# The scan's layer normalisation: from a shared job of ScalarE and GpSimd to two VectorE instructions

## The chip, the cores and the metric

The kernel runs on one core of one Trainium2 chip. The metric is the device time of one execution in microseconds. The engines are called PE (TensorE matmul), PEld (TensorE weight load), DVE (VectorE), ACT (ScalarE), POOL (GpSimd) and SP (SyncE, which here only issues DMAs).

## The reference, cut to what matters

The input `x` is 32 sequences of 256 tokens with 256 channels. A conditioned state-space block works on it first, then two layers of local attention and a gated feed-forward block work on the block's output, and `x` is added at the end. The change touches the layer normalisation in the first block alone:

```python
xc = silu(conv(x @ W_in.T + t_emb))                 # 512 channels
mu, var = xc.mean(-1), xc.var(-1)
xn = (xc - mu) / sqrt(var + 1e-05) * ln_g + ln_b    # the normalisation that is changed
Bm, Cm, dt = split(xn @ W_xproj.T, 3)               # 16 states
Ad, Bd = 1 + tanh(dt @ W_dt.T + b_dt)*0.01 * A,  Bm * min(norm(xn), 1)
h = clip(h*Ad + Bd*xn, -10, 10)                     # step by step over 256 tokens
y = (Cm . h + D*xn) * silu(gate) @ W_out.T
```

`xn` is needed by the recurrence, by the skip term `D*xn` and, through its length, by `Bd`. `Bm`, `Cm` and `dt` are not computed from `xn` but from raw sums over `xc`, corrected afterwards with two figures of each token: the reciprocal standard deviation r and the shift -mu*r.

## The kernel before, in words

**Groups and chunks.** The 32 sequences are four groups of eight (`NG`, `GB`), and the scan of a group runs over 256 time steps in eight chunks of 32 (`CH`). The state of a group is one tile of 128 partitions (16 states by 8 sequences) by 512 channels. A chunk holds 8 x 32 = 256 tokens, and so two blocks of 128 tokens (`NJ` = 2): there are 4 x 8 x 2 = 64 normalisations in all, one for each group, chunk c and block j.

**Stages.** Group 0 is scanned alone (`alone` is true for it), while TensorE also projects the inputs of the other groups ahead. After that attention and feed-forward of one group run beside the scan of the next group. At the end attention and feed-forward of group 3 run without a scan.

**What sets the order.** Every piece of work of the scan is a small function that is put into a slot with `at(slot, function, ...)`. There is one slot for each time step; `s0 = c * CH` is a chunk's first one. Attention and feed-forward have stages of their own (eight for a sequence), and the scan's slots are dealt out between them. The program that arises goes to a scheduler, which may move an instruction against others; where a call is wrapped in `tc.keep_in_program_order`, that instruction keeps its place. On the chip each engine works through its own queue in order.

**The recurrence.** `load_rows` (L685) reads one row of `xn` of eight sequences from DRAM (`xnd`), spread over the 16 states; it is put six slots ahead of its step and writes to one of six `xrep` buffers. `scale_row` (L706) multiplies it by `beta` on ACT, and `step` (L716) makes the new state on DVE with a custom instruction. `read_out` (L728) multiplies the states on PE. In group 0 two of each eight rows come from TensorE (`spread_rows`, L693) instead of a DMA.

**One normalisation before the change.** For block j of chunk c the slots are counted from s = s0 - 26 + 4j.
- s: `norm_turn` transposes the block on PE into a PSUM bank, `tp_x` (L548). All PSUM tiles of the kernel share one tag with eight banks.
- s+2: `norm_stats` takes mean and variance on DVE (L558, L560), adds epsilon (L562), takes the power -1/2 on POOL (L565) and negates the mean on DVE (L567).
- s+5: `norm_shift` makes -mu*r on ACT (L572), and `norm_apply` reads the bank on ACT and writes r*x - mu*r to the SBUF tile `xn` (L579).
- s+6: `norm_affine` multiplies `xn` by the weight `lng_sb` (L586) and adds the offset `lnb_sb` (L587), both on POOL.
- s+9: `norm_out` writes `xn` to DRAM through SP's queue (L591), and ACT squares and sums it for the length (L593).
- At s0 - 11 `length` takes the root of the sum (L599, L600). At s0 - 9 `figures` spreads r, -mu*r and the length over the tokens (L609), and at s0 - 7 `figures_in` makes `beta` and the other coefficients.

`norm_apply` and both instructions of `norm_affine` work on 128 x 512 elements, `norm_shift` on 128 x 1.

Of the kernel before, what the change touches and what calls it, by code (L numbers as in the profile page):

```python
# [10 lines left out]
FP = mybir.dt.float32  # L11
BF = mybir.dt.bfloat16
I32 = mybir.dt.int32
AF = mybir.ActivationFunctionType
ALU = mybir.AluOpType
# [4 lines left out]
P = 128  # L20
# [12 lines left out]
NJ = GB * CH // P  # L33
# [19 lines left out]
def bc(ap, axis, n):  # L53

    ap = ap.unsqueeze(axis)
    shape = list(ap.shape)
    shape[axis] = n
    return ap.broadcast_to(shape)
# [15 lines left out]
def kernel(  # L74
# [29 lines left out]
    nc = tc.nc  # L104
# [5 lines left out]
    def loaded(src, shape, name, q=None):  # L110
        t = const.tile(shape, FP, tag=name, name=name)
        (q or nc.scalar).dma_start(out=t, in_=src)
        return t
# [26 lines left out]
    lng_sb = loaded(s_ln_g.partition_broadcast(P), [P, DI], "lng_sb")  # L140
    lnb_sb = loaded(s_ln_b.partition_broadcast(P), [P, DI], "lnb_sb")
# [80 lines left out]
    def program(ctx, exact):  # L222
# [3 lines left out]
        sm = ctx.enter_context(tc.tile_pool(name="sm", bufs=2, reuse_waits="tile"))  # L226
# [7 lines left out]
        def bank(pool, tag, name):  # L234
            return pool.tile([P, DI], FP, tag=tag, name=name)
# [141 lines left out]
        def group_scan(g):  # L377
# [8 lines left out]
            alone = g == 0  # L386
# [3 lines left out]
            ck = [{} for _ in range(NCH)]  # L390

            def at(s, what, *args):
                agendas[-1].setdefault(s, []).append(partial(what, *args))
# [146 lines left out]
            def norm_turn(c, j):  # L540
                if j == 0:
                    ck[c]["xnd"] = dp.tile([GB * CH, DI], FP, tag="xnd", name="xnd")

                    ck[c]["stat"] = sm.tile([P, NJ, 3], FP, tag="stat", name="stat")
                    ck[c]["ss"] = sm.tile([P, NJ], FP, tag="ss", name="ss")
                tp = bank(ps_w, "w", "tp_x")
                for ch in range(NC_):
                    nc.tensor.transpose(  # L548
                        tp[:, ch * P : (ch + 1) * P],
                        ck[c]["xc"][:, ch, j * P : (j + 1) * P],  # L550
                        ident,
                    )
                ck[c]["tp", j] = tp

            def norm_stats(c, j):
                tp, stat = ck[c]["tp", j], ck[c]["stat"]
                st = sm.tile([P, 6], FP, tag="st", name="st")
                nc.vector.bn_stats(st, tp)  # L558
                mv = sm.tile([P, 2], FP, tag="mv", name="mv")
                nc.vector.bn_aggr(mv, st)  # L560
                ve = sm.tile([P, 1], FP, tag="ve", name="ve")
                nc.vector.tensor_scalar_add(  # L562
                    ve, mv[:, 1:2], LN_EPS if alone else 4 * LN_EPS
                )
                nc.gpsimd.tensor_tensor(stat[:, j, 0:1], ve, neg_half[:, 0:1], ALU.pow)  # L565
                nm = sm.tile([P, 1], FP, tag="nm", name="nm")
                nc.vector.tensor_scalar_mul(nm, mv[:, 0:1], -1.0)  # L567
                ck[c]["nm", j] = nm

            def norm_shift(c, j):  # L570
                stat = ck[c]["stat"]
                nc.scalar.activation(  # L572
                    stat[:, j, 1:2], ck[c].pop(("nm", j)), AF.Copy, scale=stat[:, j, 0:1]
                )

            def norm_apply(c, j):
                tp, stat = ck[c].pop(("tp", j)), ck[c]["stat"]
                xn = sp.tile([P, DI], FP, tag="xn", name="xn", bufs=2)
                nc.scalar.activation(  # L579
                    xn, tp, AF.Identity, bias=stat[:, j, 1:2], scale=stat[:, j, 0:1]  # L580
                )
                ck[c]["xn", j] = xn

            def norm_affine(c, j):
                xn = ck[c]["xn", j]
                nc.gpsimd.tensor_mul(xn, xn, lng_sb)  # L586
                nc.gpsimd.tensor_add(xn, xn, lnb_sb)  # L587

            def norm_out(c, j):
                xn = ck[c].pop(("xn", j))  # L590
# [10 lines left out]


            def figures(c):
                stat = ck[c].pop("stat")
                ck[c]["rhs"] = []
                for j in range(NJ):
                    rhs = sm.tile([P, 3, CH], FP, tag="rhs", name="rhs")
                    tc.keep_in_program_order(
                        nc.vector.tensor_mul(rhs, bc(tok_step, 1, 3), bc(stat[:, j], 2, CH))  # L609
                    )  # L610
                    ck[c]["rhs"].append(rhs)
# [244 lines left out]
            for c in range(NCH):  # L856
                s0 = c * CH
                for hb in range(CH // TB):
                    s = s0 + hb * TB
                    for i in range(NI):  # L860
                        at(s + 4 * i + 5, read_out, c, hb, i)
                    at(s + 21, gated, c, hb)
                    at(s + 25, out_gate, c, hb)
                    at(s + 11, skip, c, hb)
                for ch in range(NC_):
                    at(s0 - 38 + 2 * ch, conv_in, c, ch)
                    at(s0 - 37 + 2 * ch, conv_taps, c, ch)
                    at(s0 - 36 + 2 * ch, conv_th, c, ch)
                    if not alone:
                        at(s0 - 35 + 2 * ch, conv_out, c, ch)  # L870
                for ch, s in enumerate((13, 16, 17, 18)):
                    at(s0 + s + 2, gate_th, c, ch)
                    if not alone:
                        at(s0 + s + 4, gate_out, c, ch)
                at(s0 - 25, raw_copy, c)
                at(s0 - 24, raw_turn, c)
                for j in range(NJ):
                    s = s0 - 26 + 4 * j
                    at(s + 2, norm_stats, c, j)
                    at(s + 5, norm_shift, c, j)  # L880
                    at(s + 5, norm_apply, c, j)
                    at(s + 6, norm_affine, c, j)
                    at(s + 9, norm_out, c, j)
                at(s0 - 11, length, c)
                at(s0 - 9, figures, c)
                at(s0 - 7, figures_in, c)
                at(s0 - 6, decay_th, c)
                at(s0 - 5, decays, c)
                at(s0 - 4, put_c, c, 0)
                at(s0 + 4, put_c, c, 1)  # L890
                for d in range(KM):
                    at(s0 + 45 + 2 * d, copy_y, c, d)
                    at(s0 + 46 + 2 * d, put_y, c, d)
            agendas.append({})
            for c in range(NCH):
                s0 = c * CH
                at(s0 - 43 if alone else s0 + 6, load_x, c)
                if alone:
                    for ch in range(NC_):
                        at(s0 - 40 + 2 * ch, project, c, ch)  # L900
                else:
                    for i in range(2):
                        at(s0 - 44 + 2 * i, load_projected, c, i)
                for ch, s in enumerate((13, 16, 17, 18)):
                    at(s0 + s, project, c, NC_ + ch)
                at(s0 - 27, raw_sums, c)
                for j in range(NJ):
                    at(s0 - 26 + 4 * j, norm_turn, c, j)
                at(s0 - 8, figures_out, c)
                for t in range(CH):  # L910
                    if not by_tensor(t):
                        at(s0 + t - 6, load_rows, c, t)
                    if by_tensor(t) and t % XR == 0:
                        at(s0 + t - 4, spread_rows, c, t)
                    at(s0 + t - 2, scale_row, c, t)
                for hb in range(CH // TB):
                    s = s0 + hb * TB
                    at(s - 9 if alone else s + 7, load_skip, c, hb)
                    at(s + 23, out_turn, c)
                for d in range(KM):  # L920
                    at(s0 + 43 + 2 * d, project_y, c, d)

            if alone:
                n = (NG - 1) * NCH * 2
                for u in range(n):
                    s = -30 + u * (NCH * CH) // n
# [6 lines left out]
        def scan_slots(groups):  # L933


            slots, scans = {}, [group_scan(g) for g in groups]
            for part in range(2):
                for i, agendas in enumerate(scans):
                    for s, what in agendas[part].items():
                        slots.setdefault(i * S + s, []).extend(what)  # L940
            for s in range(min(slots), max(slots) + 1):
                for what in slots.get(s, ()):
                    what()
                yield s
# [717 lines left out]
```

## Time and profile before

| | |
|---|---|
| median of three runs | 3595.93 us (3587.54 to 3600.59) |
| profiled execution | 3582.75 us, of which the span is 3581.0 us |
| granted TensorE clock | 0.992 |
| PE busy | 3446.0 us, 96% of the span |
| PEld busy | 2253.9 us, 63% |
| DVE busy | 2667.3 us, 74% |
| ACT busy | 1998.7 us, 56% |
| POOL busy | 1892.2 us, 53% |

The first scan step (L716) of group 0 starts 47.5 us into the span, the first step of group 1 at 436.7 us, and the last step of group 3 at 2795.8 us. What comes before 40 us is the start, 40 to 440 us is the scan alone, 440 to 2700 us the scan beside attention and feed-forward, and the rest is attention and feed-forward alone.

A busy share is an average over these stages, so a stage has to be looked at by itself. PE's ends are modelled, so a PE that is shown as busy is not always one at its peak. In a line on a group of instructions the columns are: line, engine, operation, output and inputs, shape, count, then the busy time and the mean of one, then the idle time of the engine just before them with what ended it. In a line on waits they are the time in total, how often, and the longest one.

### The profile page before, as it was taken

What the parts mean: (1) busy time and instruction counts of PE and PEld (TensorE: products, weight loads), DVE (VectorE), ACT (ScalarE), POOL (GpSimd) and SP (SyncE); (2) the same over time, 40 slices, a digit from 0 to 9 for tenths busy, and PEclk for the clock granted to TensorE, in tenths of its full rate; (3) what the DMA queues carried; (4) which work ended last, traced back from release to release, by engine and by line L of the source; (5) the groups of instructions that cost most, each with busy time, mean ns of one, the idle gap of its engine ahead of it and who ended that gap; (6) DMA issues with size and microseconds to landing.
All of it is one profiled execution on the core that took longest, in us unless ns stands there. A gap on an engine that the chain in (4) does not pass through costs nothing.

```text
span 3581.0 us, 57673 instructions
## 1 busy us (share of the span) xinstructions
PE 3446.0 (96%) x20220; PEld 2253.9 (63%) x20220; DVE 2667.3 (74%) x5049; ACT 1998.7 (56%) x3599; POOL 1892.2 (53%) x1842
## 2 busy tenths in 40 slices
PE   7999989999999999999999999999999999999999
PEld 4555335666656666666666666666666677777777
DVE  5888889888788777888787778888877555555553
ACT  4666656656555665566566655655666444434442
POOL 4433477645556555655565556555544454544551
PEclk9999999999999999999999999999999999999999
DMA  7887665445354545444454555534454112011101
GB/s 207 219 221 213 198 174 149 120 117 143 109 144 125 149 141 148 130 118 127 118 142 125 138 149 140 143 106 131 114 141 122 54 50 61 13 30 38 33 27 37
DMA packets 468767, 435.68 MB, mean 122 GB/s; under 512 B 228723, under 2 KB 308084, under 8 KB 468340
## 3 DMA queue, kind: packets, MB, share of 16 engines
q1 hardware_dynamic: 384018, 419.88, 42.0%
q10 hardware_dynamic: 84450, 12.01, 2.0%
q8 instruction: 163, 2.67, 0.3%
q14 instruction: 136, 1.11, 0.1%
HBM read 383.54 MB, written 46.66 MB: 120 GB/s over the span
## 4 chain that ended last, share of the span: by engine, by line
PE 61%; DVE 19%; DMA 7%; POOL 6%; ACT 4%; issue 3%; SPq 0%; ACTq 0%; DVEq 0%; POOLq 0%
PE ps_qkv L989 13%; PE pa L1375 13%; DVE h L716 7%; PE po_f L1402 7%; DMA xrep<-xnd 5%; PE ps_wo L1039 5%; PE y L728 4%; PE ov L1271 4%; PE sc L1215 3%; PE ps_out L808 3%; PE ps_in L399 2%; PE tr_qk L1028 2%; PE rs L1252 2%; ACT xrep L706 2%; DVE acc L489 2%
## 5 line engine op out<-in xcount | busy, mean ns | idle before, releaser
L716 DVE CUSTOM_DVE_ANT_0 h<-h,xrep,lim 128x512 f32<-128x512 f32 x1024 | 961.0, 938 | 228.9 <-ACT xrep L706 196.6
L706 ACT ACTIVATE xrep<-xrep,beta 128x512 f32<-128x512 f32 x960 | 672.3, 718 | 341.4 <-DMA xrep<-xnd 219.8
L989 PE MATMUL ps_qkv<-qkv,res 128*128 128x512 f32 x1536 | 713.5, 601 | 17.9 <-DVE rinv L1260 8.4
L1375 PE MATMUL pa<-hT,w 128*128 128x256 f32 (+1 forms) x2816 | 675.1, 382 | 11.3 <-DVE zT L799 10.7
L1375 PEld LDWEIGHTS pa<-hT,w 128*128 128x128 f32 (+1 forms) x2816 | 516.9, 188 | 152.9 <-issue 35.4
L1013 POOL TENSOR_TENSOR rot<-rot,swp 128x512 f32<-128x512 f32 x256 | 339.9, 1328 | 475.3 <-DVE swp L1010 423.5
L1021 POOL TENSOR_TENSOR rn<-ss,neg_half 128x8 f32<-128x8 f32 x256 | 466.8, 1823 | 18.4 <-DVE ss L1019 7.8
L989 PEld LDWEIGHTS ps_qkv<-qkv,res 128*128 128x128 f32 x1536 | 282.2, 191 | 301.6 <-issue 241.4
L728 PE MATMUL y<-h,ly 128*32 128x512 f32 x2048 | 348.9, 609 | 16.9 <-DVE h L716 13.9
L1327 POOL TENSOR_TENSOR rstd<-ve,neg_half 128x2 f32<-128x2 f32 x64 | 46.9, 733 | 527.6 <-DVE ve L1325 511.3
L1393 DVE SCALAR_TENSOR_TENSOR ag<-pa,b_sb,ag 128x256 f32<-128x256 f32 x320 | 151.6, 474 | 222.4 <-ACT ag L1386 222.3
L1402 PE MATMUL po_f<-ag,w 128*128 128x256 f32 x1280 | 309.0, 389 | 5.9 <-DVE fo L1413 3.8
L1022 POOL TENSOR_TENSOR rot<-rot,rn 128x512 f32<-128x512 f32 x256 | 289.4, 1130 | 20.0
L1402 PEld LDWEIGHTS po_f<-ag,w 128*128 128x128 f32 x1280 | 236.8, 191 | 71.3 <-issue 12.0
L1386 ACT ACTIVATE ag<-pa,b_sb 128x256 f32<-128x256 f32 x320 | 150.2, 469 | 233.1 <-PE pa L1375 232.1
L1002 ACT ACTIVATE sq<-ps_qkv 128x512 f32<-128x512 f32 x256 | 150.8, 595 | 185.1 <-PE ps_qkv L989 119.4
L1039 PE MATMUL ps_wo<-oT,wo 128*128 128x256 f32 x1024 | 231.7, 379 | 0.5 <-DVE ag L1393 0.5
L489 DVE SCALAR_TENSOR_TENSOR acc<-xr,wc_sb,acc 128x256 f32<-128x256 f32 x384 | 195.1, 531 | 47.7 <-POOL acc L478 47.2
L1005 DVE TENSOR_TENSOR rot<-ps_qkv,rc_sb 128x512 f32<-128x512 f32 x256 | 174.8, 683 | 65.6 <-ACT sq L1002 65.0
L1039 PEld LDWEIGHTS ps_wo<-oT,wo 128*128 128x128 f32 x1024 | 194.4, 190 | 28.1 <-DVE ag L1393 0.9
L1227 ACT ACTIVATE pT<-sc 128x512 f32<-128x512 f32 x384 | 202.3, 603 | 7.6 <-PE sc L1215 5.8
L1271 PE MATMUL ov<-pT,v_sb 128*64 128x256 f32 (+1 forms) x2048 | 183.7, 330 | 19.4 <-DVE ag L1393 19.3
(160 smaller groups left out, 5482.8 us busy)
## 6 DMA issues: line engine op xcount, KB each, us to landing
xrep<-xnd SPq DMA_DIRECT2D x960, 256.0 KB
rb<-inv SPq DMA_DIRECT2D x128, 256.0 KB
xnd<-xn SPq DMA_DIRECT2D x64, 256.0 KB
qkv<-in_wqkv_dram SPq DMA_DIRECT2D x24, 512.0 KB
ahead<-xs_a SPq DMA_DIRECT2D x48, 256.0 KB
xp<-ahead SPq DMA_DIRECT2D x48, 256.0 KB
xd<-xnd SPq DMA_DIRECT2D x192, 64.0 KB
w<-in_w_dram SPq DMA_DIRECT2D x80, 128.0 KB
```

The lines of the kernel that those rows point to most:

```text
L489: nc.vector.scalar_tensor_tensor(acc, xr[:, :, k : k + CH], wc_sb[:, ch, k : k + 1], acc, ALU.mult, ALU.add,)
L706: scaled = nc.scalar.activation(bx, ck[c].pop(("bx", t), bx), AF.Copy, scale=ck[c]["beta"][:, t : t + 1])
L716: nc.vector._custom_dve(TENSOR_ADD_SAT, out=h_new, in0=state["h"], in1=bx, s0=ck[c]["lim"][:, 0, t : t + 1], s1=ck[c]["lim"][:, 1, t : t + 1],
L728: nc.tensor.matmul(ck[c]["y", hb][32 * q : 32 * q + 32, :], ly[hb % 2][:, 32 * t : 32 * t + 32], ck[c].pop(("h", hb * TB + t)), start=(i = ...
L989: nc.tensor.matmul(ps, res[b][:, k, t0 : t0 + W], wt["qkv", a][:, k], start=(k == 0), stop=(k == KM - 1),)
L1013: nc.gpsimd.tensor_add(rot, rot, swp)
L1021: nc.gpsimd.tensor_tensor(rn, ss, neg_half, ALU.pow)
L1022: nc.gpsimd.tensor_mul(rot, rot, bc(rn, 2, DH))
L1039: nc.tensor.matmul(po[:, d], wt["wo", 0][:, c, d * P : (d + 1) * P], oT[:, c, :], start=(c == 0), stop=(c == NC_ - 1),)
L1271: nc.tensor.matmul(ov[r * DH : (r + 1) * DH, i, kw * W :], self.qkv[b][2][:, kw, h * DH : (h + 1) * DH], self.p.pop((b, kw, i0 + i, r)), s ...
L1375: nc.tensor.matmul(dst[x], wt["w1", m][:, k, x], self.h[:, k], start=(k == 0), stop=(k == KM - 1),)
L1402: nc.tensor.matmul(self.po[:, d], wt["w2", 0][:, m, d * P : (d + 1) * P], self.ag[m], start=(m == 0), stop=(m == len(MCH) - 1),)
```

## The change

The two POOL instructions and the two ACT instructions of a normalisation are taken out. Two DVE instructions of the form (in0 op scalar) op in1 take their place:
- In `norm_stats`, slot s+2, DVE reads the bank and writes (x - mu) * weight to `xn`. This does not need r, so it doesn't wait for POOL's power. The bank is free after it.
- In the new `norm_scale` DVE makes `xn` * r + offset in place. It stands at slot s+5 in group 0 and at slot s+7 in the other groups, and it keeps its place in the program's order.

The negated mean (L567) goes too. Its product with r, which `figures` needs, is made for both blocks of a chunk at once by one small DVE instruction in `figures`. For that, mean and variance are kept for the chunk in a tile `mv` of 128 x 2 x 2. The power on POOL (L565), `norm_out` and all other slots stay.

```diff
             def norm_stats(c, j):
-                tp, stat = ck[c]["tp", j], ck[c]["stat"]
+                tp, stat, mv = ck[c]["tp", j], ck[c]["stat"], ck[c]["mv"][:, j]
                 st = sm.tile([P, 6], FP, tag="st", name="st")
                 nc.vector.bn_stats(st, tp)
-                mv = sm.tile([P, 2], FP, tag="mv", name="mv")
                 nc.vector.bn_aggr(mv, st)
...
                 nc.gpsimd.tensor_tensor(stat[:, j, 0:1], ve, neg_half[:, 0:1], ALU.pow)
-                nm = sm.tile([P, 1], FP, tag="nm", name="nm")
-                nc.vector.tensor_scalar_mul(nm, mv[:, 0:1], -1.0)
-                ck[c]["nm", j] = nm
-
-            def norm_shift(c, j):
-                stat = ck[c]["stat"]
-                nc.scalar.activation(
-                    stat[:, j, 1:2], ck[c].pop(("nm", j)), AF.Copy, scale=stat[:, j, 0:1]
-                )
-
-            def norm_apply(c, j):
-                tp, stat = ck[c].pop(("tp", j)), ck[c]["stat"]
                 xn = sp.tile([P, DI], FP, tag="xn", name="xn", bufs=2)
-                nc.scalar.activation(
-                    xn, tp, AF.Identity, bias=stat[:, j, 1:2], scale=stat[:, j, 0:1]
+                nc.vector.scalar_tensor_tensor(
+                    xn, ck[c].pop(("tp", j)), mv[:, 0:1], lng_sb, ALU.subtract, ALU.mult
                 )
                 ck[c]["xn", j] = xn
 
-            def norm_affine(c, j):
+            def norm_scale(c, j):
                 xn = ck[c]["xn", j]
-                nc.gpsimd.tensor_mul(xn, xn, lng_sb)
-                nc.gpsimd.tensor_add(xn, xn, lnb_sb)
+                tc.keep_in_program_order(
+                    nc.vector.scalar_tensor_tensor(
+                        xn, xn, ck[c]["stat"][:, j, 0:1], lnb_sb, ALU.mult, ALU.add
+                    )
+                )
...
             def figures(c):
-                stat = ck[c].pop("stat")
+                stat, mv = ck[c].pop("stat"), ck[c].pop("mv")
+                nc.vector.scalar_tensor_tensor(
+                    stat[:, :, 1], mv[:, :, 0], -1.0, stat[:, :, 0], ALU.mult, ALU.mult
+                )
...
                     at(s + 2, norm_stats, c, j)
-                    at(s + 5, norm_shift, c, j)
-                    at(s + 5, norm_apply, c, j)
-                    at(s + 6, norm_affine, c, j)
+                    at(s + 5 if alone else s + 7, norm_scale, c, j)
                     at(s + 9, norm_out, c, j)
```

More of the change, by code (lines that the diff above doesn't have):

```diff
@@ L545, in norm_turn @@
                     ck[c]["ss"] = sm.tile([P, NJ], FP, tag="ss", name="ss")
+                    ck[c]["mv"] = sm.tile([P, NJ, 2], FP, tag="mv", name="mv")
                 tp = bank(ps_w, "w", "tp_x")
```

## The prediction

> **What bounds the kernel now.** I read the busy table by stage first, because the page's shares mix four regimes (columns: stretch, its length, then busy us of each engine, granted clock, DMA share, GB/s).
>
> ```profile
> core 0: us, PE busy (x) PEld busy (x) DVE busy (x) ACT busy (x) POOL busy (x), PEclk, DMA share, GB/s
> 40.00:440.00 400.00, 371.59 (x1567) 187.49 (x1567) 343.64 (x616) 255.04 (x465) 163.59 (x216) 0.97 0.77 211
> 440.00:740.00 300.00, 277.68 (x1586) 158.35 (x1586) 266.42 (x483) 184.27 (x341) 189.10 (x180) 0.98 0.54 148
> 740.00:1500.00 760.00, 726.22 (x4450) 475.58 (x4447) 609.61 (x1159) 450.72 (x819) 431.89 (x420) 0.99 0.49 134
> 1500.00:2700.00 1200.00, 1171.54 (x7303) 779.52 (x7302) 960.37 (x1825) 722.23 (x1313) 687.24 (x638) 1.00 0.48 130
> ```
>
> Group 0's scan (40 to 440 us) has DVE at 86%; in this stretch the chain of work is led by DVE's scan step (23%) and the row loads (20%). From 1500 us on PE is at 98% and DVE at 80%: PE sets the pace. 440 to 1500 lies between. After 2700 no normalisation is left.
>
> Next the groups of instructions, for prices.
>
> ```profile
> L716 DVE CUSTOM_DVE_ANT_0 h<-h,xrep,lim 128x512 f32<-128x512 f32 x1024 | 961.0, 938 | 228.9 <-ACT xrep L706 196.6 <-DVE h L716 8.7 <-PE y L728 2.3
> L586 POOL TENSOR_TENSOR xn<-xn,lng_sb 128x512 f32<-128x512 f32 x64 | 92.0, 1437 | 88.4 <-ACT xn L579 88.4
> L587 POOL TENSOR_TENSOR xn<-xn,lnb_sb 128x512 f32<-128x512 f32 x64 | 88.9, 1390 | 4.4
> L579 ACT ACTIVATE xn<-tp_x,stat 128x512 f32<-128x512 f32 x64 | 49.7, 777 | 2.1 <-ACT stat L572 0.4
> L572 ACT ACTIVATE stat<-nm,stat 128x1 f32<-128x1 f32 x64 | 18.7, 293 | 148.7 <-POOL stat L565 146.6 <-DMA rw<-raw 2.1
> L567 DVE TENSOR_SCALAR nm<-mv 128x1 f32<-128x1 f32 x64 | 8.9, 140 | 0.0
> L1393 DVE SCALAR_TENSOR_TENSOR ag<-pa,b_sb,ag 128x256 f32<-128x256 f32 x320 | 151.6, 474 | 222.4 <-ACT ag L1386 222.3
> L1005 DVE TENSOR_TENSOR rot<-ps_qkv,rc_sb 128x512 f32<-128x512 f32 x256 | 174.8, 683 | 65.6 <-ACT sq L1002 65.0
> L1010 DVE TENSOR_TENSOR swp<-ps_qkv,rs_sb 128x256 f32<-128x256 f32 x512 | 191.7, 415 | 1.9 <-POOL rot L1013 1.2
> ```
>
> Then the timeline around one normalisation of group 0, DVE above POOL, for what the two engines do to each other:
>
> ```profile
> 211.69 0.80 DVE L716 CUSTOM_DVE_ANT_0 h<-h,xrep,lim 128x512 f32<-128x512 f32 x1
> 212.53 1.78 DVE L716 CUSTOM_DVE_ANT_0 h<-h,xrep,lim 128x512 f32<-128x512 f32 x1
> ...
> 212.49 1.26 POOL L586 TENSOR_TENSOR xn<-xn,lng_sb 128x512 f32<-128x512 f32 x1 [1.56 <-ACT xn L579]
> 213.84 1.60 POOL L587 TENSOR_TENSOR xn<-xn,lnb_sb 128x512 f32<-128x512 f32 x1
> ```
>
> The scan step beside L586 takes 1.78 us and not 0.80. It is no accident: the 348 scan steps that overlap no POOL instruction have a median of 0.808 us, and the stretched ones lie beside POOL's two-input instructions. DVE instructions with a PSUM input don't stretch (L779: 0.670 to 0.687 us in all 64). Summed over 40 to 440 us, what DVE instructions took over their undisturbed time beside L586 or L587 is 22.7 us (29 cases); over 440 to 2700 it is 11.3 us (15 cases).
>
> Last the waits, ACT's and SP's own:
>
> ```profile
> ACT stat L572 <- POOL stat L565: 146.6, 44, 8.3
> SPq L591 <- POOL xn L587: 149.9, 46, 7.1
> ```
>
> ACT stands 3.3 us at a time before `norm_shift`, SP as long before writing `xn`.
>
> **The change part by part.** *Prices.* The first new DVE instruction reads the bank. Its form costs 474 ns on 256 elements (L1393); 256 more cost 683 - 415 = 268 ns (L1005, L1010); so 0.742 us, and with a PSUM input it shouldn't stretch. The second reads two SBUF tensors. The same form on 256 elements has undisturbed medians of 0.418 (L773) and 0.478 us (L489), so 0.69 to 0.75; I take 0.72. It can stretch: scan steps of 440 to 2700 us gained 0.136 us on average, so I add 0.12 there. The small product in `figures` I take at 0.2 us a chunk (L656 0.164, L636 0.234, similar forms).
>
> [...]
>
> *Start (before 47.5 us), 2 normalisations.* Here the chain is bare: block 1's epsilon ends at 31.49 us, POOL's power waits behind block 0's L587 until 32.23, ACT follows at 33.49 and 34.18, POOL's two at 35.03 and 36.39, and the square starts at 37.69. After the change the power runs at 31.6 to 32.2, the second DVE instruction ends at 32.95, the square starts at 33.1: 4.6 us less. The weight sums, due at 36 us then, are ready at 35.1, close behind. I take -4 (-5 to -2).
>
> *Scan alone, 16 normalisations.* DVE gains 16 x 0.742 + 16 x 0.72 + 8 x 0.2 = 25.0 us, and loses 16 x 0.14 (L567) + 22.7 of stretch = 24.9. A draw: two POOL instructions had already cost DVE 1.4 us of each normalisation. ACT loses 16 x 1.07 = 17 us of 255; DVE waited 16.0 us for ACT's rows here, and I credit 2 of them. Row loads, with DMA at 77%, are next and keep the rest. -2 (-10 if the price is 0.69 and most of that wait goes; +11 if half the stretch comes back beside POOL's other work).
>
> *440 to 2700 us, 46 normalisations.* DVE: 46 x 0.742 + 46 x 0.72 + 23 x 0.2 + 46 x 0.12 = 77 us more, 46 x 0.14 + 11.3 = 18 less; so about 60 us, from 81% (1836 of 2260) to 84%. ACT loses 46 x 1.07 = 49 us and some 140 us of standing; POOL loses 46 x 2.8 = 130. The bank is freed after 5.7 us and not 8.4 (from the first transpose to ACT's end, against the end of L567 plus 0.742).
>
> What of it reaches PE? From 1500 us on PE's listed waits are small and elsewhere (13.7 us for L1393, 6.7 for L1260, 4.6 for L799 in 1200 us). In a steady chunk (2318 to 2420 us) they lie at 2394 and 2401, the new instructions near 2321, 2336 and 2347. The cover is the lag of the read-out: PE's `read_out` starts at the least 3.1 us, by the median 8.2 us after the last of its four steps. 1.46 us of DVE fits under 3.1; if that cover were gone, 22 normalisations would cost 32 us. So 0 (-8 to +8). Between 440 and 1500 the lag is shorter (median 4 us, a tenth at nothing, in 440 to 740), DVE is fuller, but ACT (53 us of standing) and POOL are relieved and PE has 56 us idle to win: -2 (-12 to +10).
>
> *Where the stalls go.* ACT no longer stops for the power; next late for it are the rows (139 us of waits for `xrep` DMAs in 440 to 2700). DVE now waits for the power in its own queue, with scan steps behind it, but the power ends well ahead: of block 0 of a steady chunk at 2322.0, and step s+5 starts at 2332.5, s+7 at 2335.8; in group 0, 119.2 against 120.9. So nothing. SP's `xn` write is moved past two steps; that is the second rival.
>
> Sum: -4 - 2 - 2 + 0 = -8 us. Against the profiled execution of 3582.75 that makes 3575; the median of the runs lies 13 us higher, 3595.93, and so 3588. The ends of the four terms, not all at once, give 3570 to 3604.
>
> **The rivals.**
> 1. *Relief pays (faster).* Between 440 and 1500 us ACT, POOL and banks hold PE, and half of its 56 us idle goes: 28 us, 3560. For it: ACT's waits of up to 8.3 us and DVE's 60 us for ACT's rows there. Against it: PE's own waits name many releasers, few over 5 us in total.
> 2. *SP is held (slower).* `xn` is ready only after step s+7. In a steady chunk that is 2337.3 against 2326.3 now for block 0, 2348.4 against 2343.1 for block 1. The next row load behind the write is that of step s+11, whose buffer is free after s+5; if SP's order stays, it waits two steps, 3 to 4 us, plus the 2.7 us of issuing the skip loads. It decides once rows come over 3.1 us late, beyond the lag; at 1 us of PE for each of 46, +46, 3634. Against it: the writing order is worked out anew, and in program order the first load behind the write is that of s+15, free only after s+9.
> 3. *DVE's load arrives (slower).* The start gives nothing, a third of the 60 us ends up on PE, mostly before 1500 us, where DVE is at 80 to 89%: 3616. Against it: the same lag.
>
> That the change isn't carried out as described is no case: removed and added instructions are plain.
>
> **How the numbers follow.** Forecast 0.52, rivals 0.18, 0.18 and 0.12. I call 0.5% (18 us, so 3578 and 3614) what a measurement can tell from no change. Faster: a fifth of the forecast (0.10) and rival 1: 0.28. Slower: most of rival 2 (0.15) and over half of rival 3 (0.07): 0.22. Same: 0.50. The range goes from 3562 to 3628, half-way into rivals 1 and 2, and leaves out about 0.1 on each side.
>
> **What would show it.** First scan step at 43.5 us, not 47.5; L716's mean near 0.80 to 0.83 in group 0 with next to no 1.7 us steps beside the normalisation; the new instructions at 0.74 and 0.72 us; step 1 of group 1 within 10 us of 430; DVE busy near 2725, ACT 1930, POOL 1710 us; the period of a steady chunk still 102 us. I am wrong if DVE waits for L565, if SP's waits before `xnd` grow and DVE's waits for rows with them, or if the second instruction costs over 1 us.

## The result, and the profile after

The changed kernel takes 3602.02 us (median of 20 runs, 3591.31 to 3611.23) against 3590.85 us (median of 20, 3580.93 to 3600.59; the table above had the first three of them): a ratio of 1.0029 with a 95% interval of 1.0021 to 1.0038. It is slower by 11 us. The time lies inside the range of 3562 to 3628, and the difference is under the 0.5% that was called no change; but a gain of 8 us was forecast, and the interval excludes a gain. The profiled execution has a span of 3600.3 us. The one of before, with 3581.0, comes from an execution that was 8 us quicker than the median of its runs, with a granted clock of 0.992 against 0.985 to 0.991 in the versions below, so the ratios of timed runs decide here and not single profiles.

The busy table by stage, changed kernel (columns as before):

```profile
40.00:440.00 400.00, 368.31 (x1563) 189.44 (x1561) 342.14 (x637) 240.10 (x431) 113.07 (x181) 0.95 0.78 211
440.00:740.00 300.00, 269.21 (x1526) 153.22 (x1526) 259.84 (x481) 171.66 (x312) 164.78 (x164) 0.97 0.53 144
740.00:1500.00 760.00, 729.47 (x4452) 477.06 (x4451) 621.71 (x1181) 440.00 (x795) 386.37 (x388) 0.98 0.49 135
1500.00:2700.00 1200.00, 1165.15 (x7219) 772.31 (x7219) 973.56 (x1843) 698.10 (x1259) 612.93 (x587) 1.00 0.47 129
```

The load went where it was said to go. In the scan alone DVE is at 342 us, as before (344), with 21 instructions more; ACT has 15 us less and POOL 51 us less. The last row shows a loss where PE sets the pace: in the same 1200 us PE did 7219 matmuls instead of 7303, though POOL and ACT were relieved by 74 and 24 us and DVE got only 13 us more.

The groups of instructions, changed kernel:

```profile
L710 DVE CUSTOM_DVE_ANT_0 h<-h,xrep,lim 128x512 f32<-128x512 f32 x1024 | 921.8, 900 | 114.9 <-ACT xrep L700 72.3 <-PE y L722 19.6 <-DVE h L710 5.2
L575 DVE SCALAR_TENSOR_TENSOR xn<-xn,stat,lnb_sb 128x512 f32<-128x512 f32 x64 | 50.7, 792 | 0.1
L567 DVE SCALAR_TENSOR_TENSOR xn<-tp_x,mv,lng_sb 128x512 f32<-128x512 f32 x64 | 47.3, 739 | 0.0
L603 DVE TENSOR_TENSOR rhs<-tok_step,stat 128x96 f32<-128x96 f32 x64 | 30.6, 505 | 41.9 <-POOL stat L591 41.9
L596 DVE SCALAR_TENSOR_TENSOR stat<-mv,stat 128x2 f32<-128x2 f32 x32 | 7.8, 243 | 41.5 <-POOL stat L565 41.4
```

Before the change the group of `rhs` read:

```profile
L609 DVE TENSOR_TENSOR rhs<-tok_step,stat 128x96 f32<-128x96 f32 x64 | 17.2, 308 | 2.0 <-POOL stat L600 2.0
```

The two large instructions (L567, L575) wait for nothing. The scan step fell by 39 us in all, and its wait for ACT's rows from 196.6 to 72.3 us. But two small instructions of `figures` now hold DVE: the new small product (L596) waits 41.4 us for POOL's power, and `rhs` (L603), which the change didn't touch, waits 41.9 us for POOL's root of the length, where it waited 2.0.

The waits in the steady stage, 1500 to 2700 us, changed kernel and then the kernel before:

```profile
DVE stat L596 <- POOL stat L565: 28.1, 12, 3.2
DVE rhs L603 <- POOL stat L591: 22.1, 12, 1.9
...
PE pa L1367 <- DVE zT L793: 12.0, 10, 2.1
```

```profile
PE pa L1375 <- DVE zT L799: 4.6, 4, 1.2
```

Twelve chunks lie in this stretch, and both DVE waits come once in each. PE's wait for `zT` went from 4.6 to 12.0 us. `zT` is the product with the gate that DVE makes of the scan's output while it empties the bank `tz`; `pa` is the feed-forward's matmul that needs a bank.

The timeline of one steady chunk shows how the one leads to the other. The changed kernel, and then the same place of the kernel before (start, duration, engine, line; a wait in square brackets):

```profile
2385.14 1.28 DVE L603 TENSOR_TENSOR rhs<-tok_step,stat 128x96 f32<-128x96 f32 x2 [1.84 <-POOL stat L591]
...
2390.56 1.89 PE L1367 MATMUL pa<-hT,w 128*128 128x256 f32 x8
...
2393.92 0.88 DVE L710 CUSTOM_DVE_ANT_0 h<-h,xrep,lim 128x512 f32<-128x512 f32 x1
...
2405.93 0.68 DVE L793 TENSOR_TENSOR zT<-tz,sg 128x512 f32<-128x512 f32 x1
...
2406.66 1.99 PE L1367 MATMUL pa<-hT,w 128*128 128x256 f32 x8 [0.92 <-DVE zT L793]
```

```profile
2373.00 1.89 PE L1375 MATMUL pa<-hT,w 128*128 128x256 f32 x8
...
2375.24 0.88 DVE L716 CUSTOM_DVE_ANT_0 h<-h,xrep,lim 128x512 f32<-128x512 f32 x1
...
2376.05 0.42 DVE L609 TENSOR_TENSOR rhs<-tok_step,stat 128x96 f32<-128x96 f32 x2
...
2387.59 0.68 DVE L799 TENSOR_TENSOR zT<-tz,sg 128x512 f32<-128x512 f32 x1
...
2388.33 1.99 PE L1375 MATMUL pa<-hT,w 128*128 128x256 f32 x8
```

Counted from the first `pa`, the scan step comes after 3.36 us instead of 2.24, `zT` after 15.37 instead of 14.59, and the last `pa` after 16.10 instead of 15.33. So DVE is 1.1 us late behind `rhs`, has regained a third of it by `zT`, and the remaining 0.8 us is lost on PE. The twelve chunks from step 576 to 960 say that this happens about once in each: their median length is 102.95 us against 102.16, and together they take 1237.4 us against 1227.5. `rhs` stands before the scan step now and behind it before the change: it moved in DVE's queue.

### The profile page after: what moved, and what is told of

It is laid out like the page before. It is cut to its first block, busy times and chain, and to the rows that moved or that the text cites. A ratio compares the mean times of both kernels' runs of the same rounds, so it can differ in the third digit from the quotient of the medians.

```text
span 3600.3 us, 57475 instructions
## 1 busy us (share of the span) xinstructions
PE 3450.8 (96%) x20220; PEld 2258.4 (63%) x20220; DVE 2705.5 (75%) x5145; ACT 1943.2 (54%) x3471; POOL 1703.8 (47%) x1714
## 4 chain that ended last, share of the span: by engine, by line
PE 60%; DVE 20%; DMA 7%; POOL 6%; issue 3%; ACT 3%; SPq 0%; ACTq 0%; DVEq 0%; POOLq 0%
PE pa L1367 13%; PE ps_qkv L981 12%; DVE h L710 7%; PE po_f L1394 6%; DMA xrep<-xnd 5%; PE ps_wo L1031 4%; PE y L722 4%; PE ov L1263 3%; PE ps_out L802 3%; PE sc L1207 2%; DVE acc L489 2%; PE tr_qk L1020 2%; PE ps_in L399 2%; POOL rn L1013 2%; PE rs L1244 2%
## 5 line engine op out<-in xcount | busy, mean ns | idle before, releaser
L710 DVE CUSTOM_DVE_ANT_0 h<-h,xrep,lim 128x512 f32<-128x512 f32 x1024 | 921.8, 900 | 114.9 <-ACT xrep L700 72.3
L700 ACT ACTIVATE xrep<-xrep,beta 128x512 f32<-128x512 f32 x960 | 671.8, 719 | 358.2 <-DMA xrep<-xnd 244.4
L1013 POOL TENSOR_TENSOR rn<-ss,neg_half 128x8 f32<-128x8 f32 x256 | 466.7, 1823 | 24.0 <-DVE ss L1011 13.3
L722 PE MATMUL y<-h,ly 128*32 128x512 f32 x2048 | 339.7, 611 | 22.4 <-DVE h L710 21.2
L1319 POOL TENSOR_TENSOR rstd<-ve,neg_half 128x2 f32<-128x2 f32 x64 | 54.2, 846 | 628.0 <-DVE ve L1317 611.7
```

The source lines that it names most:

```text
L700: scaled = nc.scalar.activation(bx, ck[c].pop(("bx", t), bx), AF.Copy, scale=ck[c]["beta"][:, t : t + 1])
L710: nc.vector._custom_dve(TENSOR_ADD_SAT, out=h_new, in0=state["h"], in1=bx, s0=ck[c]["lim"][:, 0, t : t + 1], s1=ck[c]["lim"][:, 1, t : t + 1],
L722: nc.tensor.matmul(ck[c]["y", hb][32 * q : 32 * q + 32, :], ly[hb % 2][:, 32 * t : 32 * t + 32], ck[c].pop(("h", hb * TB + t)), start=(i = ...
L1013: nc.gpsimd.tensor_tensor(rn, ss, neg_half, ALU.pow)
```

## The two theories

In the programs' queues `rhs` stood eight steps ahead of the chunk's first step (s0-8) in the kernel before, and stands at s0-9 to s0-12 in the changed one, with the small product still earlier, at s0-17 to s0-21. `rhs` is kept in program order and the product isn't; the scheduler put the product ahead, and `rhs`, whose predecessor on DVE in the program the product now is, was no longer held back by what preceded it before. That last clause is my reading of the queues of several versions and was not tested by itself.

**Order theory**: the loss is the place of the small product and of `rhs` in DVE's queue. **Load theory**: it is the 1.5 us more of DVE work in each normalisation (the prediction's third rival), and the waits of DVE are a by-product.

A third candidate is the granted clock. In every version a run's time goes with it (the correlation of time and clock over a version's runs lies between -0.59 in e4 and -0.94 in e9): of the changed kernel's twenty runs the quickest (3591.31 us) had 0.989 and the slowest (3611.23) 0.983. The median clock of these runs is 0.987, and 0.990 in the runs of the kernel before that were taken beside the experiments, so a part of the 11 us may come this way. It is not what separates the versions below: e5 and e10, with median clocks of 0.9875 and 0.988, lose nothing, and e9, with 0.989, is 14 us slower than these two. In the steady stage the clock is 1.00 in both tables. What lowers it before that stays open.

## The experiments

Ratios are to the kernel before, run beside each experiment in five rounds (six runs of e3, e7 and e9, twelve of each of the others).

**e1, the product kept in its place.** `rhs` is queued at s0-8 again; all else is as changed.

```diff
-                nc.vector.scalar_tensor_tensor(
-                    stat[:, :, 1], mv[:, :, 0], -1.0, stat[:, :, 0], ALU.mult, ALU.mult
-                )
+                tc.keep_in_program_order(
+                    nc.vector.scalar_tensor_tensor(
+                        stat[:, :, 1], mv[:, :, 0], -1.0, stat[:, :, 0], ALU.mult, ALU.mult
+                    )
+                )
```

> The changed kernel, with the small product of mean and r in figures (128 x 2 elements) also kept in its place in the program's order. Theory A (order): in the changed kernel this product, free to move, was put about ten scan steps ahead, and the instruction after it in figures, which keeps its place behind it, went ahead two to four steps too; DVE then stood 41 us for each of the two before POOL's powers, and this is what PE pays for. Then with the product in place the ratio to the kernel before falls from 1.003 to 0.997 to 1.000, the waits of DVE for the two powers fall from 83 us to under 10, and a steady chunk takes 102.3 us again and not 103.2. Theory B (load): the 1.46 us of DVE work of each normalisation are what PE pays for. Then the ratio stays at 1.003, whatever the order.

Measured: 3596.99 us, 1.0013 (1.0002 to 1.0025). DVE's waits for POOL's power and root are gone from the steady stage, and PE's wait for `zT` there is 7.4 us. About half of the loss is back, which settles it for neither theory.

**e2, the product alone.** The kernel before, with an extra small product that nothing uses; ACT and POOL do the normalisation.

```diff
                 stat = ck[c].pop("stat")
+                spare = sm.tile([P, NJ], FP, tag="spare", name="spare")
+                nc.vector.scalar_tensor_tensor(
+                    spare, stat[:, :, 1], -1.0, stat[:, :, 0], ALU.mult, ALU.mult
+                )
```

> The kernel before, with one more DVE instruction in figures: a product of 128 x 2 elements of the same shape, free to move, into a spare tile that nobody reads. Nothing else is changed; the normalisation stays on ACT and POOL. Theory A (order): the spread of the figures goes ahead by two to three steps as in the changed kernel, DVE stands about 40 us before POOL's power of the length, and the ratio is 1.001 to 1.004. Theory B (load): 32 instructions of 0.16 us are 5 us of DVE work; the ratio is 1.000.

Measured: 3595.69 us, 1.0018 (1.0006 to 1.0030). The waits of the steady stage:

```profile
DVE spare L606 <- ACT stat L572: 29.6, 12, 3.4
...
DVE rhs L613 <- POOL stat L600: 20.3, 11, 1.8
...
PE pa L1379 <- DVE zT L803: 11.9, 10, 2.1
```

Without any of the load, the three waits of the changed kernel are there in its sizes, and the median chunk is 102.99 us.

**e3, the load alone.** The kernel before, with DVE's two instructions added to what ACT and POOL do; the second leaves `xn` as it is.

```diff
+                xn = sp.tile([P, DI], FP, tag="xn", name="xn", bufs=2)
+                nc.vector.scalar_tensor_tensor(
+                    xn, tp, mv[:, 0:1], lng_sb, ALU.subtract, ALU.mult
+                )
...
+                tc.keep_in_program_order(
+                    nc.vector.scalar_tensor_tensor(
+                        xn, xn, one[:, 0:1], xn, ALU.mult, ALU.max
+                    )
+                )
...
+                    at(s + 5 if alone else s + 7, again, c, j)
```

> The kernel before, with the two large DVE instructions of the change as additional work: the first reads the bank and writes to xn before ACT overwrites it, the second rewrites xn in place with max(xn*1, xn) after POOL's offset, at the changed kernel's slots. ACT and POOL keep all their work and no product is added. Theory A (order): DVE's load alone does little, ratio 0.999 to 1.002 (group 0, where DVE is the bound, can pay up to 16 x 1.46 = 23 us, since POOL's stretch stays too: then 1.006, and all of it before 440 us). Theory B (load): besides group 0, PE pays about 0.8 us in each steady chunk: over 10 us more after 440 us.

Measured: 3625.67 us, 1.0101 (1.0082 to 1.0120). Group 0's 256 steps take 400.3 us (before 389.1), group 1's 748.2 (735.2), and the steady chunk has a median of 102.24, as before. The median hides something here: five of the twelve chunks are 1.2 to 1.6 us longer than their counterparts before, and the twelve together take 1234.7 us against 1227.5. So load without relief is dear in groups 0 and 1 and costs some 7 us in the steady stage too, without an early `rhs`. It isn't pure load: all three engines now write the same `xn` in turn, DVE's second instruction waited 11.7 us for the others, and 54.3 us of POOL's idle time before its product with the weight ended with DVE's `xn`. How much of the cost is load and how much these waits stays open.

**e4, group 0 alone.** The whole change, but only where `alone` is true.

```diff
+            direct = alone
...
-                    at(s + 5, norm_shift, c, j)
-                    at(s + 5, norm_apply, c, j)
-                    at(s + 6, norm_affine, c, j)
+                    if direct:
+                        at(s + 5 if alone else s + 7, norm_scale, c, j)
+                    else:
+                        at(s + 5, norm_shift, c, j)
+                        at(s + 5, norm_apply, c, j)
+                        at(s + 6, norm_affine, c, j)
```

> The change in group 0 alone; groups 1 to 3 normalise as before. By the prediction's terms the start gains 4 us and the scan alone 2 us: ratio 0.998. By theory A the product is free to move here too, so part of the scan's gain is lost to waits for POOL: 0.999 to 1.000. By theory B, with DVE's work of group 0 even: 0.999 to 1.000 too. The run shows which part of the changed kernel's 11 us arises before 440 us: 0 us by both theories.

Measured: 3588.26 us, 0.9992 (0.9980 to 1.0005), group 0 in 387.2 us. Group 0 is not where the loss is, though its product moves freely too.

After these four the product's order had been shown to cost, but e1 had won back only half. The next four ask what the rest is.

**e5, the product on GpSimd.** Nothing new stands ahead of `rhs` on DVE.

```diff
-                nc.vector.scalar_tensor_tensor(
-                    stat[:, :, 1], mv[:, :, 0], -1.0, stat[:, :, 0], ALU.mult, ALU.mult
-                )
+                nc.gpsimd.tensor_tensor(stat[:, :, 1], mv[:, :, 0], stat[:, :, 0], ALU.mult)
...
-                nc.vector.tensor_copy(wsum, tmp["tw"][:, :, 0, 0])
+                nc.vector.tensor_scalar_mul(wsum, tmp["tw"][:, :, 0, 0], -1.0)
```

> The whole change, but the small product of figures is made on GpSimd (one 128 x 2 instruction a chunk, the sign put into the weight sums once at the start), so nothing is put ahead of rhs in DVE's queue that could move; rhs is queued at step s0-8 again. Order theory: as with the product kept in place or a little better, ratio 1.000 to 1.0015, no DVE wait for POOL's power at L596 or rhs in 1500 to 2700 us, PE's wait for zT 4.5 to 7.5 us there, steps 512 to 928 in 1334 to 1340 us. Load theory: the product is only 0.2 us a chunk, so nothing is won over the whole change: 1.0025 to 1.0035, steps 512 to 928 near 1346 us.

Measured: 3590.98 us, 0.9993 (0.9982 to 1.0004). The whole loss is gone, with all of DVE's large new work still there. In the steady stage no wait of the product or of `rhs` is listed, and this is left of PE's wait for `zT`:

```profile
PE pa L1365 <- DVE zT L791: 5.3, 5, 1.7
```

**e6, groups 1 to 3 alone, the product in its place.** As e4 with `direct = not alone`, and the product kept as in e1.

> The two DVE instructions in groups 1 to 3 only, with the small product kept in its place there; group 0 is as before the change. Order theory: with rhs at its place the 48 normalisations cost nothing, 0.9992 to 1.0006, and what the version with the product in place still lost (1.0013) must come from group 0. Load theory: 1.0008 to 1.002 (3 to 7 us), groups 1 to 3 together 5 to 9 us longer than before, PE's wait for zT in 1500 to 2700 us 7 us against 4.6.

Measured: 3590.58 us, 0.9999 (0.9987 to 1.0011). In the timed runs the 48 normalisations whose cost was in dispute cost nothing, as the order theory expected. The single profile has what the load theory expected (`zT` 7.3 us, groups 1 to 3 together 2366.9 us against 2359.1), but against the quick profile of before; the timed runs count here.

**e7, the work doubled.** e1, and in groups 1 to 3 two more instructions behind the second one.

```diff
+                if not alone:
+                    for _ in range(2):
+                        tc.keep_in_program_order(
+                            nc.vector.scalar_tensor_tensor(
+                                xn, xn, one[:, 0:1], xn, ALU.mult, ALU.max
+                            )
+                        )
```

> The version with the product in place, and in groups 1 to 3 two more in-place DVE instructions of the same form and size behind the second one in each normalisation (1.5 us more of DVE for each of 48; their arithmetic leaves xn unchanged). If DVE's load is what is left of the loss, 48 x 1.5 = 72 us more of it doubles what groups 1 to 3 lose: ratio 1.003 to 1.005, steps 512 to 928 5 to 10 us longer than in the version with the product in place (1338.6). If the load is hidden by the read-out's lag and the loss lies elsewhere, 1.0008 to 1.002 and 1336 to 1342 us.

Measured: 3608.74 us, 1.0040 (1.0026 to 1.0054). The 96 instructions are 74.4 us of DVE, and by the two ratios the kernel is 0.27% (10 us) slower than e1. That is the ratio the load theory expected, but not in the expected place: steps 512 to 928 take 1334.9 us (e1: 1338.6), while group 1's steps take 747.8 us against 737.7. So further load is paid, about an eighth of it, and before 1500 us, not where PE sets the pace.

**e8, the product free in group 0 only.** e1 with the product kept only `if not alone`.

> The whole change, with the product kept in its place in groups 1 to 3 and free in group 0, where rhs then is queued three to four steps earlier. Order theory: an early rhs costs nothing where DVE sets the pace by itself (group 0 alone with a free product gave 0.9992), and costs in groups 1 to 3; so 0.999 to 1.001, group 0 in 387 to 389 us after its first step, steps 512 to 928 in 1334 to 1340 us. Load theory: no different from the version with the product in place, 1.0010 to 1.002.

Measured: 3593.24 us, 1.0005 (0.9994 to 1.0017), group 0 in 385.9 us. No harm of an early `rhs` is seen in group 0. The profiles hint at the reverse: with DVE's two instructions group 0 took 385.9 to 388.5 us where `rhs` was early (changed, e4, e8) and 390.0 to 394.5 where it stayed (e1, e5, e7, e10).

Left open was whether the product's own wait or the place of `rhs` costs.

**e9, `rhs` early and nothing else.** The kernel before with one number changed.

```diff
-                at(s0 - 9, figures, c)
+                at(s0 - 11, figures, c)
```

> The kernel before with one edit: figures is called at slot s0-11, so that rhs is queued on DVE at step s0-10 or s0-11 as in the changed kernel, and nothing is added. If rhs's early place alone is the loss: ratio 1.001 to 1.0025, a DVE wait of rhs for POOL's root of about 20 us and a PE wait for zT of about 12 us in 1500 to 2700 us, steps 512 to 928 near 1345 us. If it is the small product's own wait for POOL's power (28 us in the changed kernel, 30 in the product alone): 0.9995 to 1.0008, near 1334 us.

Measured: 3605.18 us, 1.0045 (1.0028 to 1.0062). The waits of the steady stage:

```profile
DVE rhs L609 <- POOL stat L600: 21.9, 12, 1.8
...
PE pa L1375 <- DVE zT L799: 12.2, 10, 2.1
```

They are those of the changed kernel, and the median chunk is 102.90 us. No instruction is added and none made longer by the program: the place of `rhs` alone is enough for a loss of this size.

**e10, the product early, `rhs` in place.** The changed kernel, with the product put behind `norm_scale` of block 1 and kept there (s0-14 to s0-16).

```diff
+                if j == NJ - 1:
+                    stat, mv = ck[c]["stat"], ck[c].pop("mv")
+                    tc.keep_in_program_order(
+                        nc.vector.scalar_tensor_tensor(
+                            stat[:, :, 1], mv[:, :, 0], -1.0, stat[:, :, 0], ALU.mult, ALU.mult
+                        )
+                    )
```

> The whole change, with the small product moved from figures to right behind the second DVE instruction of block 1 and kept in its place there; rhs stands at step s0-8 again, the product at s0-14 or s0-15, where POOL's power has come already. If rhs's place is what costs: as with the product on GpSimd, 0.9985 to 1.0005, steps 512 to 928 in 1334 to 1340 us, PE's wait for zT 5 to 7.5 us. If an early product costs by itself: 1.001 to 1.002.

Measured: 3591.43 us, 1.0003 (0.9992 to 1.0015), `zT` 5.0 us, median chunk 102.21. An early product that finds POOL's power ready is free as long as `rhs` stays. A product that waits for the power while `rhs` stays was not run.

Side by side (waits of 1500 to 2700 us; chunk: median of steps 576 to 960):

| version | `rhs` in groups 1 to 3 | ratio | DVE `rhs` wait | PE wait for `zT` | chunk |
|---|---|---|---|---|---|
| before | s0-8 | 1 | not listed | 4.6 | 102.16 |
| changed | early | 1.0029 | 22.1 | 12.0 | 102.95 |
| e2 product alone | early | 1.0018 | 20.3 | 11.9 | 102.99 |
| e9 `rhs` early | early | 1.0045 | 21.9 | 12.2 | 102.90 |
| e1 product in place | s0-8 | 1.0013 | not listed | 7.4 | 102.68 |
| e5 product on GpSimd | s0-8 | 0.9993 | not listed | 5.3 | 102.49 |
| e6 groups 1 to 3 | s0-8 | 0.9999 | not listed | 7.3 | 102.35 |
| e8 free in group 0 | s0-8 | 1.0005 | not listed | 7.2 | 102.47 |
| e10 product early | s0-8 | 1.0003 | not listed | 5.0 | 102.21 |

The three versions with `rhs` early have intervals above 1; of the five with the change and `rhs` in place, four include 1. What stays open: the sizes among the three early ones (e2 and e9 just touch at 1.0028 to 1.0030), and whether e1's 1.0013 is more than chance. e1 differs from e8 only in group 0, which took 393.5 us in its profile against 385.9, and e6, with group 0 unchanged, shows nothing either; so what e1 lost would lie in group 0, but the intervals of e1 and e8 overlap. The twelve steady chunks together separate the versions too: 1236.5 to 1237.9 us in the three early ones, 1228.8 to 1230.8 in the five with `rhs` in place, 1227.5 before. No version beats the kernel before: e5 at 0.9993 is the same within its interval.

## Why the prediction was wrong, step by step

**The step that failed** is the sentence "DVE now waits for the power in its own queue, with scan steps behind it, but the power ends well ahead ... So nothing", together with the price of the small product, "0.2 us a chunk". I followed the wait of `norm_scale`, and for that instruction the sentence holds: L575 waited 0.1 us in 64. For the product I counted a duration (0.243 us measured) and never asked where it would stand, nor what stands behind it. It is a free instruction put ahead of one that is kept in program order. The sum's term for 1500 to 2700 us was 0 and is about 0.8 us a chunk, 10 us over the twelve steady chunks. The steps of groups 1 to 3 together are 17 us longer in the profile (2376.4 against 2359.1). My own sign for it, "I am wrong if DVE waits for L565", came true with 41.4 us.

**The cover was the wrong one.** "1.46 us of DVE fits under 3.1", the lag of the read-out, was argued for scan steps. It held for the load: e5, e6 and e10 carry it at no cost in the timed runs. But DVE's queue also holds `zT`, which empties a bank that PE takes up 0.06 us after it ends (before: `zT` ends at 2388.27, `pa` starts at 2388.33). It has no lag to spend: what `zT` is late, 0.78 us, PE is late too, 0.77 us. I had listed that wait (4.6 us for L799) and dismissed it because the new large instructions lie 40 us and more ahead of it; `rhs` lies 20 us ahead.

**Start, -4 us: a second step that failed.** The chain before `rhs` did get shorter: the first `rhs` starts at 37.9 us, and at 41.8 in e6, whose group 0 is as before and whose first 40 us had the same granted clock (0.96; the profile of before had 1.00 there and 39.4). But PE took it up only at 40.0, since its queue held other matmuls till then (42.2 in e6, 39.8 before). The first row was ready at 47.4 (49.6 in e6, 47.4 before), and the first scan step still started at 49.8 us (49.7 in e6, 47.5 before, 43.5 forecast). The lines of DVE, changed kernel and then before, show why:

```profile
49.48 0.42 DVE L472 TENSOR_TENSOR xr<-ps_in,cond_sb 128x256 f32<-128x256 f32 x1 [3.25 <-PE ps_in L399]
49.83 0.80 DVE L710 CUSTOM_DVE_ANT_0 h<-h,xrep,lim 128x512 f32<-128x512 f32 x1
```

```profile
47.53 0.81 DVE L716 CUSTOM_DVE_ANT_0 h<-h,xrep,lim 128x512 f32<-128x512 f32 x1 [1.42 <-ACT xrep L706]
```

In the changed kernel an untouched `xr` stands ahead of the first step in DVE's queue and waits for PE; before, it stood behind the step. So what was left of the gain, about 2 us against e6, went the way of `rhs`: by a changed queue order. e4, e5, e8 and e10 have the same order. In the profiles of before, the changed kernel and e2 the first step came the later, the lower the clock of the first 40 us was: 47.5 us at 1.00, 49.8 at 0.96, 61.7 at 0.75.

**Scan alone, -2 us: "a draw" of DVE's time was right, the gain is not clear.** DVE is at 342.1 us against 343.6, group 0's steps take 388.5 us against 389.1. With the change in group 0 they range from 385.9 (e8) to 394.5 us (e7), without it, and without e3's added work, from 388.0 (e6) to 389.6 (e9). The mean scan step of this stage is 0.849 us, not the announced 0.80 to 0.83: steps over 1.5 us fell from 36 to 10 of 256, not to next to none.

**Prices: right.** The bank read takes 0.739 us (predicted 0.742), the second instruction 0.747 at the median and 0.792 on average (0.72, with 0.12 of stretch). The 64 pairs took 98.0 us, 1.53 us each; the forecast's prices, all worked out from rows of the kernel before, add up to 99.1 (64 x 1.462, and 46 x 0.12 of stretch). Busy: DVE 2705.5 (2725), ACT 1943.2 (1930), POOL 1703.8 (1710).

**440 to 1500 us, -2 us.** Group 1's steps take 739.7 us against 735.2 with `rhs` early; in e1, e5, e6, e8 and e10, 737.5 to 740.1. A gain is not seen, but the granted clock of 440 to 740 us was 0.97 in the changed kernel and 0.95 in these five, against 0.98 before. With `rhs` back in its place, e5's ratio is worth -2.5 us (-6.5 to +1.4) and not the -8 forecast.

**The rivals.** Relief (1) didn't pay: ACT's wait for the power (146.6 us) went, and its wait for row DMAs grew from 219.8 to 244.4 us, as the prediction said. SP (2) was not held: its wait for `xn` before the write fell from 149.9 us to 13.3, and DVE's wait for ACT's rows from 196.6 to 72.3. DVE's load (3) costs as a further dose (e7), in the place named for it, before 1500 us, and perhaps where nothing is relieved (e3). The direction of rival 3 came in by another way.

## What to carry to other kernels

Price a new instruction not only by its duration but by its place: look up what it is put in front of on its engine, whether that neighbour's place was held by an order that the newcomer breaks, and what each of them waits for. When a trace shows an untouched instruction waiting (here `rhs`, 2 to 42 us), compare the queue orders before explaining the loss by load. A median over chunks, and one profile at another granted clock, can hide or feign a few microseconds (e3's median hid 7, and the profile of before, at 0.992, was 8 us quicker than the median run); look at the sum and the clock too. And ask of each cover which instructions of the engine it covers: the tightest of them, here the emptying of a bank that PE takes up 0.06 us later, sets what a late engine costs.

## What was not expected of the hardware

The early `rhs` also runs longer: its mean is 505 ns against 308, its median 678 against 251. In the steady chunk shown above it starts as soon as POOL's root ends, and so does POOL's next instruction, a masking of 128 x 512 elements (L1230, two in 1.25 us from 2385.06); the two `rhs` take 1.28 us beside it instead of 0.42. Of the 33 of 64 `rhs` that took over 500 ns, 30 overlap L1230; none of the other 31 does. So an instruction that waits for another engine's small result can meet the large one that was queued behind that result. It looks like the stretch of the scan steps beside POOL's two-input instructions (1.78 us instead of 0.80 beside L586 in the kernel before), here on a DVE instruction of 96 elements a partition; whether both have one cause wasn't tested.
